# Local layers: where the feed-forward's shifted tokens stand in SyncE's queue at the first of four cells

## The chip, the core and the metric

The kernel runs on one core of a Trainium2 chip. The core's engines work side by side, each on its own list of instructions in a fixed order: TensorE (PE, matmuls; its weight loads are shown as PEld), VectorE (DVE), ScalarE (ACT), GpSimd (POOL) and SyncE (SP), which here issues the DMA transfers. They wait for each other through semaphores. SBUF is the on-chip memory, PSUM holds the results of matmuls. The metric is the device time in microseconds (us), of which the median over several runs is taken.

## The reference

The input x has 4 batches of 512 tokens with 128 features, in float32. Two blocks follow one another, each with a modulated layer norm ahead of its two parts and a gated residual sum behind them. The first block has causal attention of 16 heads with a linear bias, and a mixture of 8 experts of which two count. The second has an attention of 4 heads with a memory, and in the place of its feed-forward a stack of six local layers. Their core:

```python
def shift_tokens(t):
    a, s = jnp.split(t, 2, -1)
    s = jnp.pad(s, ((0, 0), (1, 0), (0, 0)))[:, :-1]
    return jnp.concatenate([a, s], -1)
...
q = l2norm(q) * qs
k = l2norm(k) * ksc
q = q * cos * scale + rotate_half(q) * sin * scale
k = k * cos * inv + rotate_half(k) * sin * inv
out = local_attention(q, k, v)
...
for i in range(DEPTH):
    x = attn_layer(shift_tokens(x), Wqkv[i], q_scale[i], k_scale[i], Wo[i]) + x
    x = ffn_layer(shift_tokens(x), ln_g[i], ln_b[i], W1[i], b1[i], W2[i], b2[i]) + x
return x
```

Both parts of a layer read shifted tokens: one half of the features as they are, the other half from the token before. The attention has 16 heads of 64 features and windows of 32 tokens, each of which sees itself and the window before. The feed-forward is a layer norm, a projection to 2 x 341 features, a gated gelu and a projection back.

## The kernel before, in words

Features lie on the 128 partitions, the 512 tokens of a batch along the free axis. The residual of batch b in the local layers is zT[b].

The local layers are cut into 96 cells: six layers, four batches, four groups of four heads. Cell n is layer n // 16, batch (n // 4) % 4, group n % 4, so n is a multiple of 4 at the first cell of a batch. One loop (line 1097) runs over n and writes out by hand, for four cells at once, what is issued in which order. The order in which the functions are called is the order of each engine's list; an engine waits only where it needs another's result. An iteration n does, in this order:

- scores(n, 0), line 924: mask matmuls (line 934), then the products of queries qd and keys kd (line 940), then the row maxima and the subtraction on DVE (949, 951).
- scale(n + 1), line 883: POOL multiplies the rotated keys and queries of the next cell by the inverse norms rb (line 886). gather(n + 1, 1), line 888, issues the four transfers of 128 KB that lay the keys out by heads (kd<-kr, line 899).
- weigh(n - 1, 1): the second half of the last cell's attention (989), copied out by ACT (1002).
- exponential(n, 0) on ACT (960), then norms(n + 2), line 851: matmuls over the squares, logarithm and exponential on ACT (870, 872), and four transfers that spread the result (rb<-rn, line 878). rb has one buffer, so these wait for POOL's scaling of cell n + 1.
- gather(n + 1, 0): four transfers of the queries (qd<-qr, line 899).
- project(n + 3, 0), normalise(n, 0) with line 967, rotate(n + 3, 0) (831, 841, 842, 843, 844).
- output(n - 1), line 1004, after every second cell: eight matmuls (1010) and the sum into zT (1011). At n % 4 == 0 this ends a batch's attention, and its feed-forward is queued.
- place("Z"), line 1131: if a feed-forward is queued, its first piece issues two transfers of zT into xsf, the shifted tokens (shift_in, lines 809 and 810). Then shift_in for the batch that comes next, into xs, again two transfers.
- scores(n, 1), values(n + 2) with three transfers (919 to 921), the second half of project and rotate, weigh(n, 0), turn, square and, at some cells, the tables of the next layer on POOL (line 822).
- place("D"), line 1179: the feed-forward's mean (line 1038), which is the first to read xsf. The scores of cell n + 1 stand right behind it in PE's list.

The feed-forward (feed, line 1016) is a generator whose pieces are named Z, D, N, L, X, A, B, G, C; place(name) runs the next piece if it has that name. Its pieces are spread over the four iterations that follow.

So at n % 4 == 0 SyncE's list reads: kd (4), rb (4), qd (4), xsf (2), xs (2), values (3). Transfers use eight semaphores in turn, and a transfer's issue also waits for the one eight issues earlier to have landed.

```python
for c in range(2):
    for h in range(2):
        nc.sync.dma_start(y[h::2, c, :], t[64 * c : 64 * c + 64, h, :])
...
nc.sync.dma_start(xs[0:64, :], zT[b][0:64, :])
nc.sync.dma_start(xs[64:P, 1:], zT[b][64:P, 0 : S - 1])
```

## Time and profile before

| What | Value |
|---|---|
| Median of 3 runs | 2438.05 us (2430.98 to 2448.72) |
| The profiled execution | 2452.49 us, its span 2450.7 us |
| Local layers in it | from about 660 us to the end |
| PE busy from 660 to 2435 us | 1607.6 of 1775.0 us |
| DVE, ACT, POOL busy there | 1276.9, 1165.1, 1016.3 us |
| Clock granted to PE there, and before 660 us | 0.97 and 0.89 |

The profile is that of one execution, recorded by the hardware. A line of the timeline gives the start from the span's beginning, the duration, the engine, the line of the kernel, what is written and read, and in square brackets how long the engine stood idle before it and what ended that. The list of waits gives, for who waited and for whom, the total in us, the number and the longest. Windows give, for a stretch of time, the busy time of the five units with the number of instructions, the granted clock as a share of the full one, the DMA engines' share and GB/s. For a transfer, the trace holds the time of its issue by SyncE and the marks of its landing.

### The profile page before, as it was taken

Reading aid. Unit: us, or ns where it says so; the run is one execution under the profiler, and the core shown is the slowest. Engines: PE = TensorE matmul, PEld = TensorE weight load, DVE = VectorE, ACT = ScalarE, POOL = GpSimd, SP = SyncE. Lnnn points to the kernel's source line nnn. Section 1 sums busy time; section 2 is a strip of 40 time slices with the busy share of each in tenths; the row PEclk is TensorE's granted clock in tenths of the full one; section 3 lists DMA queues with packets and bytes.
Section 4 is the critical chain, followed back from the end, with each engine's and each line's share of the span. In section 5 each row is a group of like instructions: output and inputs, shape, how many; then the busy total and the mean of one; then the engine's idle time right before and its main releaser. Section 6 shows DMA issues by size and latency. Waiting matters only on the chain.

```text
span 2450.7 us, 76498 instructions
## 1 busy us (share of the span) xinstructions
PE 2187.8 (89%) x33628; PEld 1242.4 (51%) x33628; DVE 1557.6 (64%) x2258; ACT 1402.1 (57%) x2211; POOL 1072.2 (44%) x690
## 2 busy tenths in 40 slices
PE   6889999887768899999999999999999999999996
PEld 3345454544335555555555555555555555555553
DVE  3344545333257677776777777777777777777763
ACT  1334334523245676666667666676766666677662
POOL 1000101010165475555755566555755557555550
PEclk8989999988689899999999999999999999999998
DMA  2200000000135755557555655557555675555550
GB/s 74 65 3 1 3 1 1 1 1 1 39 93 136 186 120 139 124 139 184 117 132 122 176 150 127 131 121 206 116 137 117 140 196 125 125 128 131 130 139 25
DMA packets 164760, 251.23 MB, mean 103 GB/s; under 512 B 28742, under 2 KB 90380, under 8 KB 163404
## 3 DMA queue, kind: packets, MB, share of 16 engines
q1 hardware_dynamic: 164428, 246.34, 41.5%
q8 instruction: 264, 4.33, 0.8%
q14 instruction: 68, 0.56, 0.1%
HBM read 34.27 MB, written 1.05 MB: 14 GB/s over the span
## 4 chain that ended last, share of the span: by engine, by line
PE 45%; issue 12%; DVE 10%; POOL 10%; ACT 10%; DMA 8%; SPq 4%; POOLq 0%; DVEq 0%; ACTq 0%
PE pq L831 5%; PE s L286 5%; PE po L989 4%; PE py L1010 3%; POOL kr L886 3%; PE s L940 3%; PE ye L360 3%; DVE ur L842 3%; DVE qr L841 2%; DMA xsf<-zT 2%; DMA kd<-kr 2%; PE pyf L1073 2%; PE phf L1023 2%; PE p L342 2%; SPq L899 2%
## 5 line engine op out<-in xcount | busy, mean ns | idle before, releaser
L831 PE MATMUL pq<-xs,wqkv 128*128 128x512 f32 x768 | 384.2, 624 | 29.1 <-ACT sq L849 24.2
L843 POOL TENSOR_TENSOR kr<-kr,ur 128x512 f32<-128x512 f32 x96 | 121.9, 1270 | 437.5 <-DVE ur L842 406.7
L849 ACT ACTIVATE sq<-pq 128x1024 f32<-128x1024 f32 x192 | 197.4, 1028 | 152.1 <-DVE ur L842 147.0
L843 POOL TENSOR_TENSOR qr<-qr,ur 128x512 f32<-128x512 f32 x96 | 122.3, 1273 | 261.0 <-DVE ur L842 258.6
L886 POOL TENSOR_TENSOR qr<-qr,rb 128x1024 f32<-128x1024 f32 x96 | 235.7, 2456 | 0.0
L842 DVE TENSOR_TENSOR ur<-pq,tabs 128x1024 f32<-128x1024 f32 x192 | 232.4, 1211 | 0.0
L886 POOL TENSOR_TENSOR kr<-kr,rb 128x1024 f32<-128x1024 f32 x96 | 227.8, 2373 | 7.3 <-DMA rb<-rn 7.3
L1002 ACT COPY oT<-po2b 128x256 f32<-128x256 f32 x192 | 71.5, 373 | 277.5 <-PE po2b L989 277.5
L831 PEld LDWEIGHTS pq<-xs,wqkv 128*128 128x128 f32 x768 | 136.6, 196 | 178.6 <-issue 143.2
L967 DVE TENSOR_TENSOR p<-p,sm 128x512 f32<-128x512 f32 x192 | 216.1, 1125 | 6.6
L404 ACT ACTIVATE p<-s 128x1024 f32<-128x1024 f32 (+3 forms) x160 | 104.0, 701 | 196.7 <-PE s L286 154.8
L173 POOL TENSOR_TENSOR ln_rs<-ln_rs,mhalf 128x4 f32<-128x4 f32 x16 | 16.8, 1050 | 450.9 <-DVE ln_rs L172 450.9
L910 PE MATMUL pv<-wqkv,xs 128*128 128x256 f32 x768 | 203.2, 399 | 2.2 <-DVE zT L1011 1.1
L949 DVE TENSOR_REDUCE nm<-s 128x8 f32<-128x512 f32 x192 | 131.7, 686 | 111.2 <-PE s L940 111.1
L940 PE MATMUL s<-kd,qd 64*32 64x64 f32 x12288 | 175.3, 228 | 18.8 <-DMA qd<-qr 15.3
L1023 PE MATMUL phf<-l_xc,w 128*128 128x512 f32 (+1 forms) x288 | 154.1, 648 | 39.1 <-ACT vo L917 35.1
L965 DVE TENSOR_REDUCE sm<-p 128x8 f32<-128x512 f32 x192 | 130.6, 680 | 86.6 <-ACT p L960 86.6
L989 PE MATMUL po<-pT,vo 64*64 64x32 f32 x3072 | 163.9, 224 | 16.1 <-ACT pT L976 15.7
L989 PEld LDWEIGHTS po<-pT,vo 64*64 64x64 f32 x3072 | 126.5, 137 | 99.2 <-ACT pT L976 73.6
L940 PEld LDWEIGHTS s<-kd,qd 64*32 64x32 f32 x12288 | 140.3, 107 | 64.8 <-issue 52.4
L1010 PE MATMUL py<-oT,wo 128*128 128x512 f32 x384 | 172.8, 593 | 0.0
L989 PE MATMUL po2b<-pT,vo 64*64 64x32 f32 x3072 | 161.3, 222 | 5.1 <-issue 5.1
(198 smaller groups left out, 4925.3 us busy)
## 6 DMA issues: line engine op xcount, KB each, us to landing
rb<-rn SPq DMA_DIRECT2D x384, 128.0 KB
kd<-kr SPq DMA_DIRECT2D x384, 128.0 KB
qd<-qr SPq DMA_DIRECT2D x384, 128.0 KB
ve<-vo SPq DMA_DIRECT2D x96, 256.0 KB
tabs<-in_rope_dram SPq DMA_DIRECT2D x12, 1024.0 KB
ve<-vo SPq DMA_DIRECT2D x96, 128.0 KB
wqkv<-in_Wqkv_dram SPq DMA_DIRECT2D x6, 1536.0 KB
ve<-vo SPq DMA_DIRECT2D x96, 96.0 KB
```

The costliest lines, as they stand in the source:

```text
L831: mm(pq[:, h, :], layers[l][0][:, c0 : c0 + P], shifted[b], start=True, stop=True)
L842: vec.tensor_tensor(u, d["pq"], t[:, 2 * w + 1], ALU.mult)
L843: pool_e.tensor_tensor(r[:, 0, :], r[:, 0, :], u[:, 1, :], ALU.subtract)
L849: act(d["sq", w], d.pop("pq"), AF.Square)
L886: pool_e.tensor_tensor(t, t, d["rb"][:, w, :].unsqueeze(1).broadcast_to([P, 2, S]), ALU.mult)
L910: mm(pv[:, t, :], shifted[b][:, (y + t) * P : (y + t + 1) * P], layers[l][0][:, c0 : c0 + 4 * HDW], start=True, stop=True,)
L940: mm(s[c : c + 32, w, i, :], q[r, x // 2, t0 : t0 + WIN], k[r, x // 2, t0 : t0 + GK], start=False, stop=True, skip_group_check=True,)
L949: vec.reduce_max(nm, s, axis=AX.X)
L967: vec.tensor_tensor(p, p, sm.unsqueeze(2).broadcast_to([P, UW, GK]), ALU.mult)
L989: mm(po[w][c : c + 64, x // 2, i, :], d["v"][(w + i) % 2][r, 2 * u + i // 2, 64 * x : 64 * x + 64], pT[r, i, c1 : c1 + 32], start=True, st ...
L1010: mm(py, layers[l][1][:, 2 * j - 2 + y, :], o[:, :, y % 2, :], start=(y == 0), stop=(y == 3))
L1023: mm(t[0:m], w1[:, w * DI + r0 : w * DI + r0 + m], xn, start=True, stop=True)
```

## The change

In the iterations in which n is a multiple of 4, the call that issues the four transfers of the scaled queries of cell n + 1 is moved from its place ahead of project to behind place("Z"). In the other iterations it stays. All that is computed stays the same.

```diff
             place("C")
-            if 0 <= n + 1 < NC:
+
+            if 0 <= n + 1 < NC and n % NG:
                 gather(n + 1, 0)
             if nx is not None:
                 l, b, j = cells[nx]
...
             if n > 0 and cells[n - 1][2] % 2 == 1:
                 output(n - 1)
             place("Z")
+            if 0 <= n + 1 < NC and n % NG == 0:
+                gather(n + 1, 0)
             if n + 4 < NC and cells[n + 4][2] == 0:
                 b = cells[n + 4][1]
                 shifted[b] = shift_in(b, xss[b % 2])
```

NG is 4. SyncE's list at these n then reads: kd (4), rb (4), xsf (2), qd (4), xs (2), values (3). At n = 0 there is no xsf yet, and at n = 96 no qd. The lists of the other engines keep their order; which of the eight semaphores a transfer uses changes with its place.

## The prediction

> **What bounds the kernel now.** I read the page's busy shares first, then the list of waits, then the order of time around one place of the change, engine by engine. Places and iterations are named by the loop's n; the change acts where n is a multiple of 4. Times are microseconds of the span.

> The page, busy times:
> ```profile
> span 2450.7 us, 76498 instructions
> PE 2187.8 (89%) x33628; PEld 1242.4 (51%) x33628; DVE 1557.6 (64%) x2258; ACT 1402.1 (57%) x2211; POOL 1072.2 (44%) x690
> ```
> TensorE (PE) is the nearest to full, so a wait of PE is time, unless a later wait takes it back. The local layers begin near 660. Waits for the two transfers that change places:
> ```profile
> PE lm L1038 <- DMA xsf<-zT: 36.5, 22, 3.7
> ...
> PE s L940 <- DMA qd<-qr: 15.3, 24, 1.9
> ```
> The feed-forward's first matmul waits 36.5 us in 22 waits for its shifted tokens (xsf). Counted to the weight load ahead of it and over the 23 places that have both transfers (n = 4 to 92), it is 32.2 us. The scaled queries (qd) cost 15.3 us, mostly at other n.

> Place n = 48, SyncE's queue in order of time (start, length, line, transfer):
> ```profile
> 1578.93 2.55 SPq L878 DMA_DIRECT2D rb<-rn  x4
> 1581.53 2.54 SPq L899 DMA_DIRECT2D qd<-qr  x4
> 1584.16 0.54 SPq L809 DMA_DIRECT2D xsf<-zT  x1
> 1584.74 0.60 SPq L810 DMA_DIRECT2D xsf<-zT  x1
> 1585.39 0.60 SPq L809 DMA_DIRECT2D xs<-zT  x1
> ```
> The queue does not wait here: it is issuing, about 0.65 us for each transfer, and xsf stands behind four others. The chain of waits for the same place, with the time from issue to landing:
> ```profile
> 1584.74 4.31 DMA xsf<-zT
> 1589.05 0.14 issue
> 1589.19 1.26 PE lm L1038 x2
> ```
> And what it needed had long been there. VectorE (DVE) wrote zT at 1580.46 to 1581.15:
> ```profile
> 1580.46 0.69 DVE L1011 TENSOR_TENSOR zT<-zT,py 128x512 f32<-128x512 f32 x1 [0.25 <-PE py L1010]
> ```
> That is 0.38 before qd's first issue. Over the 23 places zT is ready 0.26 to 2.00 us before qd's slot, mostly 0.39. So xsf can take that slot with no wait.

> TensorE after its last work, a transposition that ends at 1587.24:
> ```profile
> 1589.19 1.26 PE L1038 MATMUL lm<-xsf,mean_w 128*128 128x512 f32 x2 [1.95 <-DMA xsf<-zT]
> 1590.24 0.64 PE L934 MATMUL s<-wmask_b,ident_b 128*128 128x256 bf16 x2
> 1590.80 0.80 PE L940 MATMUL s<-kd,qd 64*32 64x64 f32 x36
> ```
> The scores of the next cell (line 940) follow the mask matmuls at once; they need qd.

> The same place in stretches of 3.40 us (the clock granted is the last but two):
> ```profile
> 1586.60:1590.00 3.40, 1.45 (x7) 0.76 (x6) 1.02 (x1) 2.09 (x3) 2.30 (x2) 1.00 0.55 120
> 1590.00:1593.40 3.40, 3.40 (x123) 2.58 (x125) 2.03 (x3) 0.63 (x1) 3.40 (x3) 0.50 0.35 111
> ```
> PE was busy 1.45 of 3.40, and the next 3.40 run at clock 0.50.

> **The change, part by part.** It adds and removes no instruction. On SyncE xsf moves past four issues, so it leaves 2.6 us earlier; qd moves past two, so it leaves 1.2 us later. xs, ve and all that follow keep their slots. No other queue changes its order. At n = 0 there is no xsf, at n = 96 no qd: nothing changes.

> *The wait at line 1038.* xsf's second part takes the slot of qd's second. That one landed before TensorE was free in 22 of the 23 places (0.8 to 2.7 us before); at n = 60 it landed 1.5 after. So this wait, 32.2 us, goes almost whole.

> *What is late next.* qd's last part takes the slot of xsf's last and lands when that did: 1589.05 at n = 48. The scores can't start before that. Between the first matmul's start and the scores lie 1.27 us of PE work (lines 1038 and 934) that hide the delay; with the 0.1 us between landing and start, a place gains its wait, but at most 1.33. At n = 48: the waits 1.92 become 1.33. Over the 23 places the sum of min(wait, 1.33) is **23.2** (eleven places have more than 1.3). If that cover were gone, nothing would be gained: qd would only have taken xsf's place.

> *What takes part of it back.* Two chains do not start from the place's wait and so do not move. First, in iterations n+1, DVE's normalisation at line 967 reads SBUF twice and waits while GpSimd (POOL) runs its scaling:
> ```profile
> 2163.49 2.70 DVE L967 TENSOR_TENSOR p<-p,sm 128x512 f32<-128x512 f32 x1
> ...
> 2163.27 2.37 POOL L886 TENSOR_TENSOR qr<-qr,rb 128x1024 f32<-128x1024 f32 x1
> ...
> 1596.06 0.69 DVE L967 TENSOR_TENSOR p<-p,sm 128x512 f32<-128x512 f32 x1
> ```
> At n = 81 it arrived just after POOL's operation began and lasted 2.70, to 0.55 after POOL's end; at n = 49, where POOL was done, 0.69. The rotation, the square and the next projection follow. So iteration n+1 ends no sooner than 16.76 after PE ran dry (n = 68, 80 and 84, with waits of 0.24, -0.1 and 0.1, all show it), and iteration n+2 no sooner than 34.74. Against this floor, place by place, 4.5 of the 23.2 go. Second, at n = 8, 24, 40, 56 and 72 POOL also turns a table (line 822, 2.85 us) first; there the qd of cell n+2 leaves when POOL lets it, and from PE's running dry to the scores of n+3 it takes 35.75 to 35.9 in four of them, with waits from 0.47 to 1.29. Their 4.6 go too. Left: 23.2 - 4.5 - 4.6 = **14.1**.

> In these five the earlier line 967 may also slip in between the table and POOL's scaling and push that by 0.55: 0 to 2.7 us lost, I take 1.

> *The clock.* Seven places (n = 28, 32, 44, 48, 60, 64, 76), with waits of 1.7 to 3.3, are followed at once by half-clock stretches: six of 3.4 us and one of 6.8. Half of 27.2 us is 13.6; up to the scores of n+3, less what the floor takes, 11.1. The longest wait that stays is 1.4, and no wait of 1.6 or less was followed by such a stretch. Bounds 0 and 11.1; I take 8, since another execution falls otherwise on the stretches (n = 4 and 12 waited 2.7 and 2.0 without one).

> [...]

> *Sum.* 14.1 + 8 - 1 = **21 us** off the profiled execution, 2452.5 (its span 2450.7 and 1.8 around it): 2431.5, or 0.86%. That execution is 14 us over the median of the three runs shown (2438.05; 2430.98 to 2448.72, a spread of 0.7%, so 1% is about what a measurement can tell from no change). On the median 0.86% is 21: **2417**.

> **The rivals.**

> *A, all is kept.* Waits capped at 1.33 all count (23.2), the clock gives all (13.6): 37 off, 2401. For it: iterations n+2 and n+3 are constant (17.82 and 18.74 in about half of the rounds), so what reaches them is kept. Against it: the floor above. Chance 0.10.

> *B, the gain is taken back.* The clock stretches come anyway, which leaves 14.1 - 1 = 13 off, 2425, or qd's wait and the floor eat most of that too: 0 to 13 off, 2425 to 2438, say 2433. For it: of the scores in iterations n+2 many already start within 0.6 us of their qd, so that transfer is late next. Against it: it starts from ScalarE's exponential, which follows the place's own scores and so moves along. Chance 0.28. [...]

> *C, SyncE stands still on zT.* SyncE takes its queue in order. If zT comes later than the slot, xsf blocks qd, xs, ve and the next keys. It must be late by its margin (0.39 at most places) and by the mean gain (1.0) before a place loses, so from 1.4 us later than now; at 2.5 it costs 23 x 1.1 = 25 us, 2463. For it: the margin is under 0.4 at 15 places. Against it: zT and rb both follow the same TensorE work, and the margin holds in all 23 places. Chance 0.07.

> **How the numbers follow.** Forecast (13 to 32 off) 0.55, A 0.10, B 0.28, C 0.07. One per cent is 24.4. Of the forecast's 0.55 some 0.25 lie beyond it, so faster 0.35; the rest and B make the same, 0.58; slower 0.07. The range leaves out C and half of A and takes in B's end with the runs' spread: 2400 to 2442.

> **What would show it.** In the changed profile: xsf issued right after rb, with no wait of SyncE for zT; the wait of line 1038 for xsf from 36.5 to under 6; line 940 waiting for qd at n+1, some 8 us more in all, 1.4 at most each; fewer half-clock stretches after the places; iteration n+1 ending at the floor of 16.76. The forecast is wrong if line 1038 still waits, if line 940 takes over more than 15 us, if SyncE waits at line 809, or if the half-clock stretches stay.

## The result, and the profile after

The changed kernel takes 2427.4 us (median of 20 runs, 2416.4 to 2446.4), the kernel before 2439.4 beside it (20 runs). The ratio is 0.9945, with a 95% interval of 0.9924 to 0.9966: 13.4 us less, between 8 and 19 (the two medians alone differ by 12.0). The forecast was 21.

The two profiled executions differ by more, 2450.7 to 2421.4 us of span. But 19.2 of these 29.3 lie before the first mask matmul of the local layers (708.6 and 689.4 from the start), where both kernels run the same code; TensorE was at half clock there for 174 and 126 us. The local layers, from the first mask matmul to that of cell 95, went from 1691.3 to 1681.1: **10.2 us** less. Because the part ahead of them varies like this, profiles are compared below by that stretch alone.

The page of the changed kernel, busy times:

```profile
span 2421.4 us, 76522 instructions
PE 2167.1 (89%) x33628; PEld 1232.5 (51%) x33628; DVE 1570.8 (65%) x2258; ACT 1399.5 (58%) x2211; POOL 1068.5 (44%) x690
```

PE does the same 33628 matmuls in 20.7 us less busy time; 19.6 of this lies ahead of the local layers, where it spent 48 us less at half clock. The list of waits of PE (total, times, longest):

```profile
PE s L940 <- DMA qd<-qr: 23.6, 30, 2.0
...
PE lm L1038 <- DMA xsf<-zT: 4.8, 2, 3.8
```

The wait for xsf has gone from 36.5 to 4.8, and 3.8 of this is the one at n = 96, which the change doesn't touch. The wait for qd has grown by 8.3. At place n = 48 SyncE's queue is what the diff says:

```profile
1556.91 2.56 SPq L878 DMA_DIRECT2D rb<-rn  x4
1559.57 0.55 SPq L809 DMA_DIRECT2D xsf<-zT  x1
1560.16 0.60 SPq L810 DMA_DIRECT2D xsf<-zT  x1
1560.81 2.53 SPq L899 DMA_DIRECT2D qd<-qr  x4
```

xsf follows rb at once, although VectorE finished zT only 0.44 us earlier; SyncE doesn't stand on it. PE at this place (timeline, in brackets the wait):

```profile
1565.03 1.02 PE L1038 MATMUL lm<-xsf,mean_w 128*128 128x512 f32 x2
1565.89 0.38 PE L934 MATMUL s<-wmask_b,ident_b 128*128 128x256 bf16 x2
1566.20 0.30 PE L940 MATMUL s<-kd,qd 64*32 64x64 f32 x4
1566.99 0.81 PE L940 MATMUL s<-kd,qd 64*32 64x64 f32 x60 [0.49 <-DMA qd<-qr]
```

The first matmul waits for nothing; the scores wait 0.49 for qd. In the two windows around it PE is busy 2.91 of 3.40 where it was 1.45, and the next window is no longer at half clock (the last column but two):

```profile
1564.50:1567.90 3.40, 2.91 (x86) 1.83 (x84) 1.76 (x3) 2.62 (x4) 2.25 (x2) 1.00 0.58 126
1567.90:1571.30 3.40, 3.40 (x84) 2.06 (x81) 2.67 (x6) 2.34 (x4) 3.40 (x3) 1.00 0.35 111
```

So the swap did at its places what was forecast. What it gave, place by place, from PE's running dry to the scores of cell n+3, in the two profiles:

| Places (23, n from 4 to 92) | before minus after, us | half-clock time behind them, before and after |
|---|---|---|
| the seven with a half-clock stretch before (28, 32, 44, 48, 60, 64, 76) | +18.1 | 27.3 and 0 |
| the five with a table (8, 24, 40, 56, 72) | -12.2 | 0 and 27.3 |
| the other eleven | +1.9 | 10.2 and 13.7 |

The half-clock time of the local layers is 75.1 us in both. As much as left the seven places came to the five. This is where the gain went, and n = 72 and n = 40 show how. POOL's and SyncE's lists at n = 72 (timeline of the changed kernel):

```profile
1989.25 2.84 POOL L822 TENSOR_SCALAR tabs<-tabs,prm 128x1024 f32<-128x1024 f32 x1
1992.06 2.62 POOL L886 TENSOR_TENSOR kr<-kr,rb 128x1024 f32<-128x1024 f32 x1
1994.64 2.36 POOL L886 TENSOR_TENSOR qr<-qr,rb 128x1024 f32<-128x1024 f32 x1
```
```profile
1994.71 2.42 SPq L899 DMA_DIRECT2D kd<-kr  x4
1997.23 2.58 SPq L878 DMA_DIRECT2D rb<-rn  x4
1999.85 2.55 SPq L899 DMA_DIRECT2D qd<-qr  x4
```

The table (line 822) stands ahead of the scaling of cell n+2; kd leaves when its scaling is done, and rb and qd stand behind kd. At all five places qd leaves when it did before the change, 13.5 to 13.8 us after PE ran dry. The scores of n+2 are now reached earlier (their mask matmuls start 15.78 us after PE ran dry, before 17.27), and wait for qd. The timeline of PE:

```profile
2003.23 0.30 PE L940 MATMUL s<-kd,qd 64*32 64x64 f32 x4 [0.76 <-DMA qd<-qr]
2004.37 0.81 PE L940 MATMUL s<-kd,qd 64*32 64x64 f32 x60 [0.83 <-DMA qd<-qr]
...
2008.49 0.31 PE L989 MATMUL po2b<-pT,vo 64*64 64x32 f32 x1 [2.37 <-issue]
```

Over the five places this wait for qd went from 4.2 to 9.9 us. At n = 40 it was 1.31 and 0.95 us. That left PE 1.14 us of work in a window of 3.40, and the next window ran at half clock (windows of the changed kernel):

```profile
1437.50:1440.90 3.40, 1.14 (x64) 0.75 (x64) 0.71 (x1) 2.40 (x4) 2.61 (x3) 1.00 0.91 219
1440.90:1444.30 3.40, 3.40 (x101) 2.54 (x90) 1.39 (x2) 1.07 (x3) 3.40 (x2) 0.50 0.18 48
```

At n = 8 and 24 it is the same: 1.5 and 2.0 us of waiting for qd in the window ahead of the half clock. At n = 56 and 72 it is not. There the window ahead holds 1.7 and 1.4 us of an idle time for which the trace names no engine and no transfer (the line at 2008.49; see the last section), and of the waiting for qd nothing at n = 56 and 0.27 us at n = 72:

```profile
2004.10:2007.50 3.40, 1.76 (x115) 1.58 (x115) 1.38 (x2) 0.49 (x1) 3.40 (x3) 1.00 0.38 119
2007.50:2010.90 3.40, 2.41 (x26) 1.08 (x26) 0.00 (x0) 1.83 (x3) 3.40 (x3) 0.50 0.02 5
```

In the kernel before, a stretch of this length around the two waits for qd of n = 72 (0.80 and 0.62) held 1.99 of 3.40, and the clock stayed full; the idle time of the other kind was not there (at n = 56 it was, with 1.6 us, and no half clock followed):

```profile
2030.40:2033.80 3.40, 1.99 (x70) 1.30 (x70) 1.54 (x2) 3.23 (x5) 1.78 (x2) 1.00 0.60 151
2033.80:2037.20 3.40, 3.40 (x108) 2.20 (x92) 1.81 (x3) 2.00 (x4) 3.40 (x2) 1.00 0.17 52
```

### The profile page after: what moved, and what is told of

Its sections match the earlier page's. It is cut to its first block, busy times and chain, and to the rows that moved or that the text cites. A ratio compares the mean times of both kernels' runs of the same rounds, so it can differ in the third digit from the quotient of the medians.

```text
span 2421.4 us, 76522 instructions
## 1 busy us (share of the span) xinstructions
PE 2167.1 (89%) x33628; PEld 1232.5 (51%) x33628; DVE 1570.8 (65%) x2258; ACT 1399.5 (58%) x2211; POOL 1068.5 (44%) x690
## 4 chain that ended last, share of the span: by engine, by line
PE 45%; issue 13%; ACT 10%; DVE 10%; POOL 9%; SPq 7%; DMA 6%; POOLq 0%; DVEq 0%; ACTq 0%
PE pq L831 6%; PE s L286 4%; PE po L989 4%; POOL kr L886 3%; PE phf L1023 3%; SPq L899 3%; DVE ur L842 3%; PE py L1010 3%; PE pyf L1073 3%; PE ye L360 2%; PE s L940 2%; SPq L878 2%; DMA qd<-qr 2%; DVE qr L841 2%; PE pv L910 2%
## 5 line engine op out<-in xcount | busy, mean ns | idle before, releaser
L831 PE MATMUL pq<-xs,wqkv 128*128 128x512 f32 x768 | 390.3, 632 | 30.0 <-ACT sq L849 24.6
L967 DVE TENSOR_TENSOR p<-p,sm 128x512 f32<-128x512 f32 x192 | 227.8, 1187 | 6.6
L886 POOL TENSOR_TENSOR kr<-kr,rb 128x1024 f32<-128x1024 f32 x96 | 229.1, 2386 | 6.5 <-DMA rb<-rn 6.5
L886 POOL TENSOR_TENSOR qr<-qr,rb 128x1024 f32<-128x1024 f32 x96 | 230.7, 2403 | 0.0
L173 POOL TENSOR_TENSOR ln_rs<-ln_rs,mhalf 128x4 f32<-128x4 f32 x16 | 16.8, 1049 | 442.2 <-DVE ln_rs L172 442.2
L940 PE MATMUL s<-kd,qd 64*32 64x64 f32 x12288 | 173.2, 225 | 27.1 <-DMA qd<-qr 23.6
L940 PEld LDWEIGHTS s<-kd,qd 64*32 64x32 f32 x12288 | 138.7, 106 | 71.5 <-issue 46.4
L1010 PE MATMUL py<-oT,wo 128*128 128x512 f32 x384 | 172.8, 593 | 0.0
```

The lines of the kernel that those rows point to most:

```text
L831: mm(pq[:, h, :], layers[l][0][:, c0 : c0 + P], shifted[b], start=True, stop=True)
L886: pool_e.tensor_tensor(t, t, d["rb"][:, w, :].unsqueeze(1).broadcast_to([P, 2, S]), ALU.mult)
L940: mm(s[c : c + 32, w, i, :], q[r, x // 2, t0 : t0 + WIN], k[r, x // 2, t0 : t0 + GK], start=False, stop=True, skip_group_check=True,)
L967: vec.tensor_tensor(p, p, sm.unsqueeze(2).broadcast_to([P, UW, GK]), ALU.mult)
L1010: mm(py, layers[l][1][:, 2 * j - 2 + y, :], o[:, :, y % 2, :], start=(y == 0), stop=(y == 3))
```

## The experiments

The columns from the profiles are those of one execution each, in us. "Behind the seven, the five" is the half-clock time within 33 us of the first matmul of those places.

The clock can also be read over many executions, since every run on record has its span and its mean granted clock. The clock is either 1.0 or 0.5 in every profile here, so 2 x (1 - clock) x span is a run's time at half clock, ahead of the local layers and in them; half of that is an estimate of what it costs where PE is busy throughout (in the profile of the kernel before, line 831's matmuls follow one another at 0.43 us at full clock and 0.92 at half, medians of 361 and 8). The 56 runs of the kernel before, on three chips, spent 235 us at half clock (standard error 3, the uncertainty of a mean) and take 2326.6 (0.6) without half of it, on each chip the same within 2 us; the 20 runs of the changed kernel 237 (5) and 2311.2 (0.7). So the change saves 15 us that are not clock, and no clock, within some 6 us of half-clock time.

| Kernel | ratio to the kernel before, 95% interval | local layers, us | half clock in them | behind the seven, the five | waits for xsf, for qd |
|---|---|---|---|---|---|
| before | 1 | 1691.3 | 75.1 | 27.3, 0 | 36.5, 15.3 |
| the change | 0.9945 (0.9924 to 0.9966) | 1681.1 | 75.1 | 0, 27.3 | 4.8, 23.6 |
| e1 change but at the five | 0.9934 (0.9906 to 0.9961) | 1686.2 | 81.9 | 0, 13.7 | 8.8, 18.1 |
| e2 change at the five alone | 1.0027 (1.0000 to 1.0055) | 1710.4 | 109.2 | 17.1, 17.1 | 29.8, 21.0 |
| e3 PE kept busy | 1.0015 (0.9989 to 1.0041) | 1703.6 | 81.9 | 6.8, 0 | 13.0, 15.9 |
| e4 change, tables later | 0.9882 (0.9849 to 0.9916) | 1666.7 | 58.0 | 0, 0 | 3.8, 10.0 |
| e10 the same again | 0.9876 (0.9837 to 0.9915) | 1667.1 | 61.4 | 0, 0 | 3.8, 11.1 |
| e5 tables later alone | 0.9884 (0.9844 to 0.9924) | 1673.8 | 61.4 | 3.4, 0 | 27.9, 11.0 |
| e11 the same again | 0.9929 (0.9899 to 0.9960) | 1674.3 | 64.8 | 3.4, 0 | 28.3, 10.4 |
| e6 queries ahead of norms | 0.9873 (0.9835 to 0.9911) | 1656.7 | 41.0 | 13.7, 0 | 20.8, 0.6 |
| e9 that and tables later | 0.9838 (0.9799 to 0.9876) | 1663.0 | 54.6 | 0, 0 | 13.2, 0 |
| e8 change, queries early elsewhere, tables later | 0.9802 (0.9765 to 0.9840) | 1653.0 | 44.4 | 0, 0 | 3.8, 3.2 |
| e12 the same again | 0.9816 (0.9785 to 0.9847) | 1650.2 | 41.0 | 0, 0 | 3.8, 4.3 |

### The places apart

The first two kernels split the 23 places, to see whether the five with a table give the gain back.

```diff
+            moved = n % NG == 0 and (n % 16 != 8 or n == 88)   # e1
+            moved = n % 16 == 8 and n != 88                    # e2
-            if 0 <= n + 1 < NC and n % NG:
+            if 0 <= n + 1 < NC and not moved:
                 gather(n + 1, 0)
...
-            if 0 <= n + 1 < NC and n % NG == 0:
+            if 0 <= n + 1 < NC and moved:
                 gather(n + 1, 0)
```

> The change is made at 18 of the 23 places; at the five where POOL also turns a table (n = 8, 24, 40, 56, 72) the queries stay ahead. Theory T (the five table places lose 12 us in the changed kernel, because the scores of cell n+2 get to their queries before POOL has let them go, wait there and are followed by half-clock stretches): the loss goes, 20 to 30 us faster than before, ratio 0.988 to 0.992. Rival S (the missing gain is lost a little at every place, by the floor and by late instruction pages): 18/23 of what the change gave, 8 to 13 us faster, ratio 0.9945 to 0.997.

> The change is made at the five table places alone. Theory T: 7 to 15 us slower than before, ratio 1.003 to 1.006, with waits of 1 to 2.5 us of line 940 for qd at n+2 in all five and half-clock stretches behind them. Rival S: these places gain their small share, 1 to 4 us faster, ratio 0.998 to 0.9995.

The change at the five places alone gave 1.0027 (1.0000 to 1.0055): nothing gained, and by the middle of the interval 6.6 us lost. The small gain that rival S expects lies outside the interval; the loss is a little under what theory T expects, and the interval doesn't exclude the forecast's count, at most 2.7 us lost. Its runs spent 247 us at half clock (standard error 6), those of the kernel before on the same chip 233 (3), and take the same without half of it (2326.0 and 2327.3): what these places lose is clock, as far as twelve runs can tell. The change at the other places gave 0.9934 (0.9906 to 0.9961), 16 us, which lies between the two ranges and can't be told from the 0.9945 of the whole change. Its profile says why leaving out the five helps so little: they lost time there too, with the order of before. At n = 40 the scores of n+2 waited 1.20 and 1.06 us for qd and a half-clock stretch of 6.8 followed, although qd left 13.5 us after PE ran dry, as in the kernel before; its last transfer landed 1.5 us later than there, and why was not tried. At n = 56 the half clock follows an idle time of 1.5 us of the other kind. So the five places stood close to the edge in the kernel before, and it isn't only the swap at the place itself that pushes them over. The idle times that rival S puts down to late instruction pages end 1.0 to 1.7 us after a 16-KB packet of an instruction queue (last section): 15.7 us in eight of them in the profile of the kernel before, 20.4 in ten in that of the changed kernel. That pages came late in them was not shown.

### The clock by itself

Two matmuls that nobody reads were added ahead of line 1038 for the feed-forwards of batches 2 and 3 (twelve places), in the order of before. They keep PE busy while it waits for xsf.

```diff
+            if b >= 2:
+                for _ in range(2):
+                    mm(pm, mean_w, zT[b], start=True, stop=True)
```

> The order of before; ahead of line 1038, in the feed-forwards of batches 2 and 3 (n % 16 = 12 and 0), two matmuls of 0.56 us each on data that is there fill 1.1 us of the wait for xsf; their result is overwritten. The wait and the issue order stay. Theory K (a wait of 1.7 us or more makes the next 3.4 us run at half clock): the stretches right behind these places go, 6 to 13 us faster than before, ratio 0.995 to 0.9975. [...]

At the places themselves it did what it was to do. At n = 48 PE's wait would have begun at 1581.21; the stretch from there is full now (windows, e3), and the next one runs at full clock:

```profile
1581.30:1584.70 3.40, 3.40 (x72) 1.56 (x70) 0.98 (x2) 1.67 (x4) 3.03 (x3) 1.00 0.65 174
1584.70:1588.10 3.40, 3.40 (x102) 2.13 (x85) 2.44 (x5) 2.64 (x5) 3.40 (x2) 1.00 0.19 45
```

None of these places up to n = 92 has a half-clock stretch within 8 us, where the seven had one before (the 6.8 in the table comes some 20 us later). That the partly idle windows brought the half clock at these places is shown by this. But the ratio is 1.0015 (0.9989 to 1.0041): no gain, where theory K expects 0.995 to 0.9975, although the stretches behind the places went. A pair of the added matmuls takes 1.88 us, not the 1.1 that was expected and about as long as the waits that it fills, so only the clock could have been won. Over the twelve runs the half-clock time is 8 us less than that of the kernel before on the same chip (225 and 233, standard errors 7 and 3), not clear of noise, while the time without half of it is 10 us more (2337.4 and 2327.3, 1.1 and 0.7). In the profile, where the half clock of the local layers was 81.9 and not less than 75.1, idle times that weren't filled took more, and half clock followed them:

```profile
1401.00:1404.40 3.40, 0.00 (x0) 0.00 (x0) 0.00 (x0) 2.53 (x3) 1.48 (x1) 1.00 1.07 309
1404.40:1407.80 3.40, 2.91 (x14) 1.11 (x15) 0.94 (x2) 0.46 (x2) 0.00 (x0) 0.50 1.01 196
```

Here PE stood for 4.74 us, waiting for no engine and no transfer. Such idle times of over 0.9 us took 23.6 us in this profile and 15.7 before, which would account for most of the 10. Why they were longer was not tried.

### The tables out of the way

If POOL's table is what holds qd at the five places, it has to move. It is turned one iteration later, behind the scaling: in the changed kernel (e4, e10) and in the kernel before (e5, e11).

```diff
+        owed = []
         for n in range(-4, NC + 1):
...
                 scale(n + 1)
                 gather(n + 1, 1)
+            while owed:
+                rotations(*owed.pop(0))
...
-                        rotations(l + 1, w, h)
+                        owed.append((l + 1, w, h))
```

> The changed kernel, and POOL turns the tables one iteration later, behind its scaling of the keys and queries and not ahead of it (20 operations of 2.85 us). Theory T: POOL lets the queries go 2.85 us earlier at the table places, these lose nothing and gain some: 22 to 34 us faster than before, ratio 0.986 to 0.991. Rival S: the gain stays that of the change, 8 to 18 us, ratio 0.9925 to 0.997, or less where a table now stands in the way of DVE's normalisation or POOL's rotation.

> The order of before, with POOL's tables turned one iteration later, behind its scaling. Theory T (the change is worth 20 to 25 us where no table holds POOL's queries back, and the tables alone are worth little, because ahead of the change the wait for xsf already holds the table places): 2 to 9 us faster than before, ratio 0.996 to 0.999. Rival U (most of the 29 us of the changed kernel with later tables comes from the tables, whatever the order of the queue): 12 to 20 us faster, ratio 0.992 to 0.995.

With the change the ratio is 0.9882 (0.9849 to 0.9916), 29 us. The same stretch at n = 72 in the profile of e4, POOL, then SyncE:

```profile
1990.37 2.37 POOL L886 TENSOR_TENSOR kr<-kr,rb 128x1024 f32<-128x1024 f32 x1
1992.69 2.36 POOL L886 TENSOR_TENSOR qr<-qr,rb 128x1024 f32<-128x1024 f32 x1
1995.02 3.29 POOL L822 TENSOR_SCALAR tabs<-tabs,prm 128x1024 f32<-128x1024 f32 x1
```
```profile
1998.74 2.54 SPq L899 DMA_DIRECT2D qd<-qr  x4
```

Counted from the weight load of the feed-forward's first matmul (1987.18 here, 1986.04 in the changed kernel) qd leaves 11.6 us after it instead of 13.8. The scores of n+2 don't wait for it, and the place takes 35.04 to the scores of n+3 instead of 39.96. No half-clock stretch stands behind any of the five, in either profile. At n = 56 and 72 the idle times of the other kind are small in both as well (0.7 us at most); that the tables' place did this is not shown.

What wasn't expected is that the tables alone gave as much: 0.9884 (0.9844 to 0.9924), where theory T had 0.996 to 0.999 and rival U 0.992 to 0.995, in which only the repeat below lies. The tables are turned in the iterations before n = 12, 28, 44, 60 and 76 too, and had made the waits for xsf there longer. Place n = 28 of the kernel before, POOL, SyncE and PE:

```profile
1214.34 2.85 POOL L822 TENSOR_SCALAR tabs<-tabs,prm 128x1024 f32<-128x1024 f32 x1
...
1219.47 2.81 POOL L886 TENSOR_TENSOR qr<-qr,rb 128x1024 f32<-128x1024 f32 x1
```
```profile
1222.30 2.56 SPq L878 DMA_DIRECT2D rb<-rn  x4
1224.91 2.54 SPq L899 DMA_DIRECT2D qd<-qr  x4
1227.54 0.54 SPq L809 DMA_DIRECT2D xsf<-zT  x1
```
```profile
1231.48 1.09 PE L1038 MATMUL lm<-xsf,mean_w 128*128 128x512 f32 x1 [2.14 <-DMA xsf<-zT]
```

rb has one buffer and waits for the end of the scaling at 1222.28; the table ahead of that scaling, 2.85 us, delays rb, and xsf stands behind rb. In the kernel with the tables later alone PE waits less at this place, and no half clock follows:

```profile
1203.49 1.10 PE L1038 MATMUL lm<-xsf,mean_w 128*128 128x512 f32 x2 [1.40 <-DMA xsf<-zT]
```

The waits at n = 12, 28, 44, 60 and 76, which fell to 1.2 to 1.8 in the two profiles from 2.0 to 3.3, are five of the longest that the swap had been forecast to remove. So part of what the swap gains was to be had without it, and it remained to measure what the swap is worth once the tables are gone. Both kernels were run again, side by side on one chip:

> The change with the tables one iteration later, beside the next kernel on the same chip. If the swap is worth what the places of the two profiles say (about 7 us in the sum over the places), its ratio is 0.003 below that of the next. If the swap is worth nothing once the tables are out of the way, the two are within 0.001.

> The tables one iteration later without the change. If the swap is worth the 7 us, 0.003 above the run before this; if it is worth nothing, within 0.001 of it.

They gave 0.9876 and 0.9929. The one over the other, from the 6 and 11 times of the two, is 0.9961 (0.9925 to 0.9996 by resampling the times): the swap still saves 9.5 us, between 1 and 18. The profiles agree twice over: the local layers are 7.1 us shorter with the swap in the first pair (1673.8 and 1666.7) and 7.2 in the second (1674.3 and 1667.1). In the first round each ratio had been taken against a kernel before of its own, on another chip, and intervals of 0.35% to either side don't show a difference of 0.4%. Without half of the half clock, the runs of the second pair differ by 8 us (2305.1 and 2313.2, standard errors 2.2 and 1.7): what the swap saves here is waiting.

### The queries ahead of the norms

Another answer to the same wait: qd goes right behind kd at every n, ahead of rb.

```diff
                 gather(n + 1, 1)
+                gather(n + 1, 0)
...
-            if 0 <= n + 1 < NC:
-                gather(n + 1, 0)
```

> Another order, at every n: the queries qd right behind the keys kd, ahead of the norms rb; xsf stays behind all of them. qd waits for the same scaling that rb waits for, so it leaves 1 to 3 us earlier; rb leaves up to 2.6 us later and is needed some 4 us after it lands; xsf leaves about 1.5 us earlier where ScalarE held rb. If the place in the queue is what counts: the wait of line 1038 falls to under 15 us and that of line 940 for qd to under 5, 12 to 28 us faster, ratio 0.9885 to 0.995. If rb is what is late next: POOL's scaling waits for rb (some 20 us in all) and the kernel gains nothing or loses, ratio 0.998 to 1.006.

The ratio is 0.9873 (0.9835 to 0.9911). That is a little better than the range of "the place in the queue is what counts", though the wait for xsf fell only to 20.8 and not under 15. PE hardly waits for qd any more (0.6 us), and there is no half clock behind the five, although the tables stand where they stood; four stretches remain behind the seven, where xsf still stands behind kd, qd and rb. So with the order of the tables as before, qd ahead of rb does more than xsf ahead of qd.

The next kernel (e7) was to add the later tables to this, but leaves something out: the call that issues qd stands inside the added loop, so that the queries' transfers are issued for 20 cells only. The scores of the other cells read the queries before they are laid out by heads.

> The order of the run before this one, with POOL's tables one iteration later. If the tables cost only where the queries stand behind them in time: the same as without (they leave early there anyway), ratio 0.9875 to 0.9945. If POOL's hold on the table places counts by itself: 4 us or more better than without them.

It took 1.0221 (1.0180 to 1.0263), longer although it does less: the scores now hold the tile of the queries itself, and VectorE's line 841, which writes the next queries there, waits 113 us for PE's scores. It says nothing on its question. Mended:

> The queries are issued right behind the keys at every n, ahead of the inverse norms, and POOL turns the tables one iteration later, behind its scaling; nothing is left out. If the two gains are separate (each alone gave a ratio of 0.987 to 0.988), they add up to 0.976 to 0.979, with all places near 34 from PE's running dry to the scores of n+3. If they are the same gain found twice (the queries come earlier, whether the table or the norms are taken out of their way), it is 0.983 to 0.988, the table places being no better than without the turn.

The ratio is 0.9838 (0.9799 to 0.9876), in the range of "the same gain found twice". All five places take 50.4 to 50.5 us from the scores of n to those of n+3 here, as in e4, and 49.7 in e6, where the tables stand where they stood. So once qd leaves early, the later tables cost these places 0.7 us each: the scores of n+2 come 16.8 us after PE ran dry, in e6 15.8. The author puts this down to line 967, which would come behind POOL's scaling there again, as before the change (1.82 us instead of 0.69 at n = 72). Two ways of letting qd leave earlier don't add up.

### The best of the parts together

xsf first at the places of the change, qd ahead of rb at the other n, the tables later:

```diff
                 gather(n + 1, 1)
+                if n % NG:
+                    gather(n + 1, 0)
+            while owed:
+                rotations(*owed.pop(0))
...
-            if 0 <= n + 1 < NC and n % NG:
-                gather(n + 1, 0)
```

> The changed order at n a multiple of 4 (norms, xsf, queries), the queries ahead of the norms at the other n, and the tables later. If line 940's remaining waits and near misses at the other n cost time: 30 to 38 us faster than before, ratio 0.9845 to 0.988. If they cost nothing: as the changed kernel with later tables, 0.987 to 0.990; if rb is late, less.

> The change at n % 4 == 0, the queries ahead of the norms at the other n, the tables later. It differs from the first kernel of this group by the order at n % 4 == 0 alone: there xsf goes ahead of the queries. If the first matmul's wait for xsf (20.8 us in the profile of the kernel with the queries ahead of the norms) is still time at the end, it is 0.003 to 0.008 below the first; if the wait is taken back later, within 0.001 of it. Against the kernel before 0.978 to 0.983, as measured once.

The ratios are 0.9802 (0.9765 to 0.9840) and 0.9816 (0.9785 to 0.9847): some 45 us less than before, more than the 30 to 38 expected for e8, and faster than the change alone. The page of e8:

```profile
span 2400.4 us, 76942 instructions
PE 2156.1 (90%) x33628; PEld 1225.4 (51%) x33628; DVE 1588.7 (66%) x2258; ACT 1399.8 (58%) x2211; POOL 1071.0 (45%) x690
```

Against e9 on the same chip, which has qd ahead of xsf at the places and is the same otherwise, e12 stands at 0.9978 (0.9939 to 1.0013): whether the swap still helps in this company is not settled by time. In the profiles the local layers are 12.8 us shorter with it, but 6.8 of this is half of the difference in half-clock time (54.6 and 41.0), which varies from one execution to the next. The six runs of each differ by 0.3 us without half of the half clock (2300.9 and 2301.2, standard errors 1.0 and 1.5), which speaks for "taken back later".

## Why the prediction was right, and where it was not

The direction was right: the gain is real, and under 1%. The number, 21 us, was 8 too high by the ratio (13.4, interval 8 to 19). That is at the upper end of rival B, "the clock stretches come anyway", 13 off; and B is what the traces and the runs show. That the time, 2427, lies between 2400 and 2442 says little for the forecast's own mechanism, since that range took in B's end.

- **The wait at line 1038.** Right. It was to fall from 36.5 to under 6 and fell to 4.8, with SyncE waiting for zT only at n = 96 (4.7 us), as before. Rival C, SyncE blocked, is out: the margins held.
- **What is late next.** Right in kind and size. qd at n+1 was to take about 8 us and 1.4 at most; it took 7.8, and 1.57 at most at one place.
- **The floor.** Right, but not at the five. At n = 16, 32, 36, 48, 64, 80 and 88 the scores of n+2 come 16.75 to 16.77 us after PE ran dry, forecast 16.76; and with the tables later the scores of n+3 come at 34.73 to 34.77 at thirteen of the places (e4), forecast 34.74. At the five places with a table the scores of n+2 come after 15.78 to 15.98, sooner than the forecast's soonest.
- **The five table places: the step that failed.** They were to lose 1 us, at most 2.7, by line 967 slipping in ahead of POOL's scaling. It did slip in at all five, at n = 72 at 1991.77, 0.32 us before the table's end, and took its usual 0.69; the scaling behind it took 2.62 instead of 2.36. Before, line 967 came second there, at 2020.70, 1.08 us after the scaling's start, and took 1.82. In the whole profile of the changed kernel the 102 operations of line 967 that don't overlap a scaling take 0.69 to 0.82, the 90 that do 0.69 to 2.70, in the median 1.62. The 0.32 us beside the end of the table show no delay of line 967. This push was the small part. With line 967 done before the scaling, the scores of n+2 came 1.3 to 1.5 us sooner, below the floor, while their qd left when it had left before. The prediction had seen that this qd "leaves when POOL lets it" and counted it as a gain that isn't made. It left out that PE then waits longer in one place, 9.9 us for 4.2, and that such waits have a price in clock: 17.1 us at half clock behind n = 8, 24 and 40, at most 8.5 us of time. The 10.2 us behind n = 56 and 72 follow idle times that are not waits for qd, and their cause stays open. Together the five lost 12.2 us in the profile, and 6.6 (0 to 13) when they alone were changed.
- **The clock: mis-sized by its whole amount.** The sum had 8 us from the seven places. These did lose their stretches, all 27.3 us, and gained 18.1 together. But the total stayed at 75.1, and over the 56 and 20 runs at 235 and 237, so the term came out at nothing. This and the point before are one loss, counted by place and by kind: without the clock 14.1 - 1 = 13 us was forecast, and 10.2 came in the profiles, 15 over the runs. The rule behind the term, that "no wait of 1.6 or less was followed by such a stretch", looked at single waits, and what counted here is the idle time in a window: at n = 40 waits of 1.31 and 0.95 us stood in one, and half clock followed. By the prediction's own sign, that it is wrong "if the half-clock stretches stay", this term was wrong.
- **The sum by places.** For the 18 places without a table 14.1 + 8 = 22 was forecast, and 20.0 came. For the five, -1 was forecast and -12.2 came. The remaining 2.4 of the 10.2 lie outside these stretches.
- **Rival B's counter-argument.** It was said that the transfer of cell n+2 "moves along" with the place. That holds where only ScalarE's exponential is ahead of it, and fails where POOL has a table to turn first.

What isn't settled: how often the five places fall to half clock, which by the author's estimate depends on how the grid lies (last section) and is seen in single executions only; and why the idle times that name no engine grew at n = 56 and 72.

## What to carry to other kernels

When a wait is taken away, follow the work that it had covered to the next thing that doesn't move: here a transfer two iterations on, held by an operation of another engine (POOL's table) that has nothing to do with the place of the edit. A forecast of time regained must then price the new wait with its clock, not only the old one. Taking the fixed thing out of the way was worth about as much by itself as the reordering (0.9884 and 0.9929 against 0.9945), and more together with it (0.9882 and 0.9876).

## What the runs showed of the hardware

| PE busy in a window at full clock | windows | followed by half clock |
|---|---|---|
| under 1.40 us | 117 | 117 |
| 1.40 to 1.60 | 53 | 46 |
| 1.60 to 1.80 | 75 | 32 |
| 1.80 to 2.03 | 74 | 10 |
| over 2.03 | 5820 | 0 |

So windows with 1.4 to 2.03 us of work were followed by half clock in 88 of 202 cases, those with less always and those with more never. Windows at half clock were followed by full clock in 190 of 201 cases when PE was busy for 3.0 us or more of the 3.4, and in none of 24 with under 2.8. A wait of under 1.38 us alone leaves over 2.03 us of a window to work, and none of the 5820 windows with that much was followed by half clock; the two waits in one window at n = 40 (1.31 and 0.95 us, 1.14 busy) were. What a gap of some 2 us brings is not told by its length alone: at n = 4 of before a line of the grid parts a wait of 2.71 us in 1.77 and 0.94, the window ahead of the line has 1.64 of work, and no half clock followed; at n = 64 a wait of 1.76 stood in one window with 1.65 of work, and half clock followed. The author's estimate from the table is that it depends on how much of the gap falls in one window. The grid doesn't lie alike in two executions: its first line behind the first mask matmul comes 0.76 us after it in the profile of before and 0.55 in that of the changed kernel. That would explain why stretches moved about between kernels that are alike.

**TensorE stands at times, often at the same places of its list.** In five profiles (before, the change, e3, e4, e10) PE stands for 0.9 to 4.7 us, 8 to 10 times from the first mask matmul on, 16 to 24 us in all, with no engine and no transfer named ("issue", as in the line at 2008.49 above). All 44 of these gaps end 1.0 to 1.7 us after the end of a 16-KB packet of a queue that the page lists as instruction (1.2 to 1.6 us in the profiles of before and the change). By chance 4 of 44 would, since there are 231 such packets in the local layers, one in 7.3 us. The gaps also come back at the same places of PE's list: counted in matmuls from the first mask matmul, the 44 stand at 18 places, and four of these (2214, 7170, 17082 and 22038, multiples of 4956 apart) have a gap in all five kernels, though in e3 the matmuls added ahead have shifted the work that stands there by up to 32 matmuls. So what these gaps share is the place in the list, and not what is computed there. The page has the queue (packets, MB, share of 16 engines):

```profile
q8 instruction: 264, 4.33, 0.8%
```

The longest gap, 4.74 us in e3, ends at 1404.89, 0.49 us into the stretch at clock 0.50 shown above. In the profile of the changed kernel half clock began within 1.3 us of the end of five of the ten gaps (the longest 3.68), in that of the kernel before at three of eight: 0.8 us behind those of 1.40 and 2.09, and 1.3 ahead of the end of the one of 4.00. That PE waits for its instructions in these gaps was read by the author from the times and the places; no run took the cause away.
